# In-place normalization and ELU, fewer joint key-value rows in the second group, and a place per tile in a planned two-layer graph-attention kernel

## The chip, the cores and the metric

The kernel runs on one core of one Trainium2 chip, and the time is the device time of that core in microseconds (us). The engines are TensorE (PE in the profile, with its weight loads as PEld), VectorE (DVE), ScalarE (ACT), GpSimd (POOL) and SyncE (SP). POOL issues the DMAs that take their addresses from an index (gathers and scatters), SP issues the plain ones. All engines run their own instruction streams in order and meet at semaphores. "L870" means line 870 of the kernel before.

## What is computed

The input is `x` (8 batches of 2048 nodes with 256 features) and one 0/1 adjacency matrix of 2048 x 2048, in which a node has some 5 to 24 neighbours. Two layers follow each other, each wrapped as `x = layernorm(x + layer(x))`:

```python
# layer 0, 4 heads of 64; softmax inside chunks of 256 nodes
q, k, v = x @ Wq.T + bq, x @ Wk.T + bk, x @ Wv.T + bv
scores = where(mask == 0, -10, clip(q . k / 8, -10, 10))
ctx = sum over chunks of softmax(scores in the chunk) @ v
out = layernorm(ctx @ Wo.T + bo + x) * gamma + beta
# layer 1, graph attention
Wh = h @ W;  e = leaky_relu(a_src . Wh_i + a_dst . Wh_j, 0.2)
h_out = elu(softmax(where(adj, e, -inf)) @ Wh)
```

## The kernel before, in words

**Sparse form.** The first stage (`edge_lists`) reads the adjacency matrix, makes a list of neighbours for each node, and sorts the nodes by degree into 16 tiles of 128 nodes. A tile t has `CAPS[t]` slots, 24 for the first tile and 14 down to 5 for the others. A neighbour that is not among the slots has the constant score, and its share is put in by a correction. The batches are handled in two groups of four; group 0 and group 1 are called p=0 and p=1.

**Layer 0 of a group** begins with its tables (`tables`, L736 to L749): keys and values of all 16 row tiles are computed on PE, the keys evicted by DVE (L741), the values by ACT (L746), and both written to `kv_d[p]` by SP. A key row and its value row lie next to each other, 4096 bytes each. Only when all rows are written can the gathers of that group start. Then for each tile: `fetch_x` (a gather on POOL), `query` (PE, ACT), the gather of key rows, `scores0` (a product on DVE, L947, then transposes L960, an ACT copy L963 and a product with `sel` on PE, L967), `softmax0`, the gather of value rows, `context0` (each gathered row is weighed in place by its attention and the rows are summed on PE by transposes, L879), and `finish0` (output projection, two normalizations, the rows for layer 1, a write of x1 and a scatter of Wh).

**Joint rows.** For a few slots of a tile, key row and value row are fetched by one DMA of 8192 bytes a partition (`gather_both`, L840) in place of two of 4096 (L827). How many: `min(S_ % 2 + 2 * COMBO[p], S_)` of the `S_` slots. A joint row fills one buffer of the ring by itself, while two single rows share one. From among the joint rows `apart0` takes up to `SHARE[S_]`, and those are weighed by ACT, in 16 instructions of 64 columns (L861); all others are weighed by DVE (L870), two rows in one instruction of 2048 columns where they share a buffer, and one row of 1024 columns otherwise.

**Layer 1** gathers Wh rows for a tile (`fetch1`), makes the softmax, weighs and sums (`context1`), and ends with `finish1`: transposes on PE (L1138), ELU with an exp on ACT (L1142) and two DVE instructions (L1143, L1145), a normalization, and four scatters to the output (L1149). Tiles 0 to 7 are done for each group by itself, tiles 8 to 15 for both groups together. The eight single tiles of group 0 run interleaved with layer 0 of group 1.

**The order** is not written out by hand. Every operation is entered into a plan with an engine, an estimated cost, what it reads and writes, the buffers that it takes from a named room, and a due time; `schedule` then walks through the plan once, when the kernel is built, and on each engine starts the operation with the earliest due time that is ready and finds its buffers free. The result is the fixed order of each engine's instructions. The due times come from constants: `FIRST` and `WHENT` for the tables, one integer place per tile plus `WHEN0` for layer 0, `ORDB`, `ORDC`, `ORDJ` plus `WHEN1` and `WHENJ` for layer 1. Rooms that matter here: "u" with 7, later 14, ring buffers for two gathered rows each; "b" with 10 buffers of one row of 1040 floats; "x" with 18 small ones; "gr", a count of two loads of x1 under way.

**Buffers of the results.** `finish0` takes a new "b" buffer for its result (`o = pl.new("b")`), while the context lies in another (`cT`). `finish1` takes two new ones, `xr` for the x1 row and `y` for the result, while its context lies in `hT`.

Of the kernel before, what the change touches and what calls it, by code (L numbers as in the profile page):

```python
# [17 lines left out]
P = 128  # L18
# [22 lines left out]
GH = G * H  # L41
WW = GF + GH
EMIN = 4.5399929762484854e-05
RING, BIG, MID, WIDE, SMALL, BANKS, HALVES = 10, 10, 6, 4, 18, {"m": 2, "acc": 2}, {"al": 2, "pr": 1, "sc": 1}
PAIRS = 4
GATES = {"ga": 3, "gx": 2, "gq": 3, "gr": 2}
WHENT = (-24.15, 4.05)
WHEN0 = ((-4.55, -2.2, -1.95, -1.15, -0.85, -0.15, 0.1, 0.45, 4.85, -0.05, 0.8, 1.9, 2.1, 1.25, 3.9), (-2.15, -0.4,
         -1.35, -0.6, 0.6, -0.4, 0.75, 0.65, 1.15, 0.9, 0.9, 1.15, 2.1, 1.8, 3.55))
WHEN1 = ((-0.6, -0.5, -0.1, -0.15, 0.25, 0.4, 0.8, 2.35), (-1.4, -1.15, -1.05, -2.65, -0.7, -0.4, 1.25, 1.55))  # L50
NB = 32
ROWS = (3, 6, 9, 12)
DOTS = ((1, 3), ())
COMBO = (1, 1)
SHARE = {5: 0, 6: 0, 7: 2, 8: 2, 9: 2, 10: 2, 11: 2, 12: 2, 13: 3, 14: 4, 24: 4}
SHARE1 = {5: (), 6: (), 7: (1,), 8: (1,), 9: (2,), 10: (2,), 11: (2,), 12: (2,), 13: (2, 5), 14: (2, 5), 24: (2, 5, 8)}
JOINT = (8, 9, 10, 11, 12, 13, 14, 15)
SHAREJ = {9: (2, 4, 6), 8: (2, 4, 6), 7: (2, 4), 6: (2, 4), 5: (1, 3)}
WHENJ = (-1.4, -0.8, -0.45, -2.2, -0.7, -0.2, 0.65, 1.5, 0.95, 1.75)
ORDB = (2.5, 4.5, 6.5, 8.5, 10.5, 12.55, 14.5, 16.65)  # L60
ORDC = (3.85, 4.0, 7.3, 7.0, 6.7, 9.1, 11.5, 13.0)
ORDJ = (3.1, 5.4, 6.2, 7.8, 9.2, 10.35, 12.2, 13.95)
LATE = 4
FIRST = (-39.0, 2.0, 1.0, 0.0, -40.0, -31.25, -31.15, -38.6, 1.05)
COPY = (6.0, 12.0)
TUNED = ("FIRST", "WHENJ", "ORDB", "ORDC", "ORDJ")

# [36 lines left out]
class Plan:  # L106
# [43 lines left out]
    def schedule(self):  # L150
        import collections
        import heapq
        engines = ("PE", "DVE", "ACT", "POOL", "SP")
        cand = {e: [] for e in engines}
        free = {e: 0.0 for e in engines}
        for o in self.ops:
# [316 lines left out]
def sparse_path(ctx: ExitStack, tc: tile.TileContext, keep, x, adj, Wq, bq, Wk, bk, Wv, bv, Wo, bo, gamma, beta, W, a,  # L473
# [55 lines left out]
    def kept(name, shape, dt=F32):  # L529
        return Buf(phys=const.tile(shape, dt, name=name))  # L530
# [11 lines left out]
    xs = [kept(f"xs{p}", [P, GK, NT]) for p in range(NP)]  # L542
    shift = [kept(f"shift{p}", [P, KC, G]) for p in range(NP)]
    lift = [kept(f"lift{p}", [P, KC, G]) for p in range(NP)]
    room = ctx.enter_context(tc.tile_pool(name="room", bufs=1))
    for tag, n, shape in (("u", RING - 3, [P, UNIT, WW]), ("b", BIG, [P, WW]), ("s", MID, [P, 384]), ("h", WIDE, [P, 256]), ("x", SMALL, [P, 128])):
        pl.rooms[tag] = Room([room.tile(shape, F32, name=f"{tag}{k}") for k in range(n)], tag == "u")
# [256 lines left out]
              w=[(mv, k, k + 1)])  # L804
        return mv

    def normalized(dst, src, srcs, n=G):
        mv, nm = moments(src, srcs, n), pl.new("x")
        rs = rsqrt(mv, n, "y")
        V(C_TINY, lambda: nc.vector.scalar_tensor_tensor(nm.t[:, 0:n], mv.t[:, 0:2 * n].rearrange("p (b k) -> p b k", k=2)[:, :, 0],  # L810
                                                        -1.0, rs.t[:, 0:n], op0=ALU.mult, op1=ALU.mult), r=[mv, rs], w=[nm])
        for k in range(n):
            S(c_act(F, 2), lambda k=k: nc.scalar.activation(batches(dst)[:, k, :], src(k), AF.Identity, scale=rs.t[:, k:k + 1],  # L813
                                                            bias=nm.t[:, k:k + 1]), r=[srcs(k), rs, nm], w=[(dst, k, k + 1)])

    def flat(u):
        return u.t.rearrange("p s w -> p (s w)")
# [120 lines left out]
    def scores0(p, t):  # L938
        S_ = CAPS[t]
        q = got["q", p, t][1]  # L940
        units = got["k", p, t] + got["both", p, t]
        scs = [pl.new("sc")] + [pl.new("al") for _ in range(S_ > 16)]
        scv = lambda sl: scs[sl // 16].t[:, sl % 16 * GH:(sl % 16 + 1) * GH]
        for k, (u, items) in enumerate(units):
            slots, offs = [s for s, _, _ in items], [o for _, _, o in items]
            for o in offs:
                V(c_tt(GF), lambda u=u, o=o: nc.vector.tensor_tensor(  # L947
                    by_feature(flat(u)[:, o:o + GF], "j b"), by_feature(flat(u)[:, o:o + GF], "j b"), by_feature(q.t, "b j"), op=ALU.mult),
                  r=[q], w=[(u, o, o + GF)])
            if k in DOTS[p]:  # L950
                for s, o in zip(slots, offs):
                    V(55 + 1.06 * GF, lambda u=u, s=s, o=o: nc.vector.tensor_reduce(
                        scv(s), flat(u)[:, o:o + GF].rearrange("p (j e d) -> p e j d", j=NJ, d=DP), axis=AX.XY, op=ALU.add),
                      r=[(u, o, o + GF)], w=[(scs[s // 16], s % 16, s % 16 + 1)])
                continue
            pr, prT, m = pl.new("pr"), pl.new("h"), len(slots)
            for k, o in enumerate(offs):
                def turn(u=u, o=o, k=k, pr=pr):
                    for j in range(NJ):
                        nc.tensor.matmul(pr.t[:, k * P:(k + 1) * P], flat(u)[:, o + j * P:o + (j + 1) * P], ident,  # L960
                                         is_transpose=True, start=(j == 0), stop=(j == NJ - 1), skip_group_check=True)
                T(c_tr(8), turn, r=[(u, o, o + GF)], w=[(pr, k, k + 1)])
            S(c_act(m * P), lambda pr=pr, prT=prT, m=m: nc.scalar.copy(prT.t[:, 0:m * P], pr.t[:, 0:m * P]), r=[pr], w=[prT])  # L963

            def sums(prT=prT, slots=slots):
                for k, s in enumerate(slots):
                    nc.tensor.matmul(scv(s), prT.t[:, k * P:(k + 1) * P], sel, start=True, stop=True, skip_group_check=True)  # L967
            T(c_mm(m, 16), sums, r=[prT], w=[(scs[s // 16], s % 16, s % 16 + 1) for s in slots])
        st["s", p, t] = scs
# [41 lines left out]
    def finish0(p, t):  # L1011
        cT = st.pop(("c", p, t))
        (xg, gate), xT = got.pop(("x", p, t)), got.pop(("q", p, t))[0]
        o = pl.new("b")
        pos = []
        for half in range(2):
            po = pl.new("m")
# [15 lines left out]
        for b in range(G):  # L1033
            V(c_tt(F), lambda b=b: nc.vector.scalar_tensor_tensor(batches(o)[:, b, :], first(b), mv.t[:, 2 * b:2 * b + 1], gamma_r,
                                                                  op0=ALU.subtract, op1=ALU.mult), r=[pos[b // 2], mv, ga_b],
              w=[(o, b, b + 1)])
        rs = rsqrt(mv, G, "y")
        for b in range(G):
            V(c_tt(F), lambda b=b: nc.vector.scalar_tensor_tensor(batches(o)[:, b, :], batches(o)[:, b, :], rs.t[:, b:b + 1],
                                                                  batches(xg)[:, b, :], op0=ALU.mult, op1=ALU.add),  # L1040
              r=[rs, xg, gate], w=[(o, b, b + 1)], two=True)
        normalized(o, lambda b: batches(o)[:, b, :], lambda b: (o, b, b + 1))
        Q(lambda: nc.sync.dma_start(x1_d[p][t * P:(t + 1) * P, :], rows(o)), ROW, r=[o], w=[(x1_b[p], t, t + 1)])

        xT1, wh = pl.new("b"), pl.new("b")
# [85 lines left out]

    def finish1(p, t):
        hT = st.pop(("h", p, t))
        xr, y, gate = pl.new("b"), pl.new("b"), pl.new("gr")
        Q(lambda: nc.sync.dma_start(rows(xr), x1_d[p][t * P:(t + 1) * P, :]), ROW, r=[(x1_b[p], t, t + 1)], w=[xr, gate])
        for half in range(2):
            ph = pl.new("m")
            T(c_tr(4), lambda half=half, ph=ph: [nc.tensor.transpose(ph.t[:, c * P:(c + 1) * P], cols(hT)[:, 4 * half + c, :], ident)  # L1138
                                                 for c in range(4)], r=[(hT, 4 * half, 4 * half + 4)], w=[ph])
            hv = lambda b, half=half: b.t[:, 512 * half:512 * half + 512]  # L1140
            yk, xk = (y, 2 * half, 2 * half + 2), (xr, 2 * half, 2 * half + 2)
            S(c_act(512), lambda hv=hv, ph=ph: nc.scalar.activation(hv(y), ph.t, AF.Exp), w=[ph, yk])  # L1142
            V(601, lambda hv=hv, ph=ph: nc.vector.scalar_tensor_tensor(hv(xr), ph.t, 0.0, hv(xr), op0=ALU.max, op1=ALU.add),  # L1143
              w=[ph, xk])
            V(601, lambda hv=hv: nc.vector.scalar_tensor_tensor(hv(y), hv(y), 1.0, hv(xr), op0=ALU.min, op1=ALU.add),  # L1145
              r=[xk, gate], w=[yk])
        normalized(y, lambda b: batches(y)[:, b, :], lambda b: (y, b, b + 1))
        for b in range(G):
            Pq(C_DGE, lambda b=b: nc.gpsimd.indirect_dma_start(  # L1149
                out=out_v[t * B + p * G + b],  # L1150
                out_offset=bass.IndirectOffsetOnAxis(ap=nodeb.t[:, t, p * G + b:p * G + b + 1], axis=0),
                in_=batches(y)[:, b, :], in_offset=None), r=[(y, b, b + 1), nodeb], size=P * F * 4)

    for p, v0, dv in ((0, *FIRST[:2]), (1, *WHENT)):
        for c2 in range(NCH):
# [37 lines left out]
            pl.stage(v + w[6 + 2 * k], v + w[7 + 2 * k])  # L1193

    for k in range(NT):
        layer0(k, 0, k)
    early = [t for t in range(NT) if t not in JOINT]
    for k in range(NT):
        layer0(NT + k, 1, k)
    pairs_of = wj_d.rearrange("(n k) w -> n k w", k=NP)  # L1200
    for c in range(NT):
        Q(lambda c=c: nc.sync.dma_start(pairs_of[c * P:(c + 1) * P, 0, :], wh_d[c * P:(c + 1) * P, :]), 2 * P * WW * 4, r=[wh_b[0]],
# [438 lines left out]
```

## Time and profile before

| | us |
|---|---|
| median of the three runs | 2289.88 (2281.02 to 2292.70) |
| the profiled execution's own time | 2311.25 |
| its span, first to last instruction | 2309.5 |
| first key gather of group 0 | 214.85 |
| last scatter of layer 0, group 1 (L1063) | 1817.6 |

| engine | busy us | instructions | mean ns of one |
|---|---|---|---|
| PE matmul | 1830.4 | 12215 | |
| DVE | 1756.1 | 3262 | |
| ACT | 1184.1 | 4401 | |
| POOL | 1213.3 | 1160 | |
| L861, ACT weighing (all buffers) | 501.9 | 2016 | 345, and 249 from one to the next |
| L840, joint gathers | 80.1 | 80 | 1000 |

The DMA engines were busy for about 77% of the span and moved 275 GB/s on average. Times in the trace count from the first instruction. A row of the timeline gives the start, the length, the instruction and, in brackets, the engine's idle time before it and what ended that time. A row of the waits gives the waiting engine and line, what released it, and the total, the number and the longest of these waits. "Issue" stands for idle time without a visible cause.

### The profile page before, as it was taken

The page shows a single profiled execution, that of the slowest core. Times are in us where ns is not written, and L with a number is a line of the kernel's source. Part 1 is how long each engine was busy: PE and PEld are TensorE (multiplying, and loading weights), DVE is VectorE, ACT ScalarE, POOL GpSimd, SP SyncE. Part 2 cuts the span into 40 slices and gives each one's busy share as a digit, 9 for nine tenths or more (in the row PEclk, how much of TensorE's full clock was granted, in tenths as well). Part 3 has the DMA queues.
Part 4 walks back from the last instruction along what each step waited for, and adds up shares of the span by engine and source line. Part 5 has one row for each costly group of instructions (what it writes and reads, how often), then busy time and mean ns, then how long its engine had stood idle before and what let it go on. Part 6 is the DMA issues. An engine that isn't in the chain of part 4 may idle for free. (4 is left out here: it accounts for less than half of the span.)

```text
span 2309.5 us, 36948 instructions
## 1 busy us (share of the span) xinstructions
PE 1830.4 (79%) x12215; PEld 1627.8 (70%) x12215; DVE 1756.1 (76%) x3262; ACT 1184.1 (51%) x4401; POOL 1213.3 (53%) x1160
## 2 busy tenths in 40 slices
PE   6788699788887888897778888888988766776644
PEld 4577588677777777786767777787877656665534
DVE  8923367787888788877668878888887588878965
ACT  6633445235443545523344644555563658655656
POOL 6674114735454453457446564565554555665644
PEclk9899799989998999999889999999999878887767
DMA  8858578778887786766888888888887689978662
GB/s 304 296 188 293 199 249 287 291 261 301 304 281 277 269 309 242 264 234 226 312 330 313 290 310 300 285 310 292 310 293 267 225 307 353 322 289 318 208 217 81
DMA packets 187066, 635.56 MB, mean 275 GB/s; under 512 B 35082, under 2 KB 53388, under 8 KB 171120
## 3 DMA queue, kind: packets, MB, share of 16 engines
q0 software_dynamic: 137552, 505.18, 61.5%
q1 hardware_dynamic: 46608, 126.24, 14.9%
q10 hardware_dynamic: 2708, 1.71, 0.3%
q8 instruction: 99, 1.62, 0.3%
q14 instruction: 99, 0.81, 0.1%
HBM read 596.19 MB, written 109.71 MB: 306 GB/s over the span
## 5 line engine op out<-in xcount | busy, mean ns | idle before, releaser
L879 PE MATMUL acc<-ident,u 128*128 128x128 f32 x2856 | 384.1, 286 | 44.1 <-DVE u L870 29.1
L879 PEld LDWEIGHTS acc<-ident,u 128*128 128x128 f32 x2856 | 345.2, 150 | 60.3 <-DVE u L870 34.5
L861 ACT ACTIVATE u<-u,s 128x64 f32<-128x64 f32 x1344 | 333.1, 345 | 29.6 <-DVE s L1001 21.3
L870 DVE TENSOR_TENSOR u<-u,h 128x2048 f32<-128x2048 f32 (+1 forms) x175 | 321.3, 1849 | 0.3
L947 DVE TENSOR_TENSOR u<-u,q 128x1024 f32<-128x1024 f32 x224 | 264.3, 1209 | 46.0 <-PE q L682 27.7
L827 POOL DMA_INDIRECT u<-kv_d,idv x170 | 179.5, 1056 | 173.5 <-PE h L960 65.2
L827 POOL DMA_INDIRECT u<-kv_d,idk x168 | 171.9, 1023 | 178.9 <-PE h L960 64.2
L960 PE MATMUL h<-ident,u 128*128 128x128 f32 x1456 | 199.5, 286 | 26.8 <-DVE u L947 16.5
L960 PEld LDWEIGHTS h<-ident,u 128*128 128x128 f32 x1456 | 175.4, 151 | 36.3 <-DVE u L947 19.8
L963 ACT COPY h<-h 128x256 f32<-128x256 f32 (+1 forms) x172 | 56.8, 330 | 271.4 <-PE h L960 170.2
L1149 POOL DMA_INDIRECT out_dram<-b,nodeb x128 | 135.2, 1056 | 87.8 <-ACT b L813 54.2
L879 PE MATMUL acc<-ident,at 128*128 128x128 f32 x1208 | 157.9, 282 | 23.8 <-DVE at L870 16.8
L813 ACT ACTIVATE b<-b,x,x 128x256 f32<-128x256 f32 x256 | 136.3, 597 | 68.8 <-DVE x L810 52.6
L1055 PE MATMUL m<-wa,b 128*128 128x264 f32 x512 | 147.0, 427 | 25.8 <-ACT b L1061 10.5
L879 PEld LDWEIGHTS acc<-ident,at 128*128 128x128 f32 x1208 | 141.5, 146 | 29.0 <-DVE at L870 19.9
L967 PEld LDWEIGHTS h<-sel,h 128*128 128x128 f32 x546 | 82.3, 203 | 99.3 <-ACT h L963 60.4
L967 PE MATMUL h<-sel,h 128*128 128x16 f32 x546 | 85.0, 260 | 76.8 <-ACT h L963 47.0
L870 DVE TENSOR_TENSOR at<-at,h 128x2048 f32<-128x2048 f32 (+1 forms) x74 | 141.1, 1913 | 0.1
L947 DVE TENSOR_TENSOR at<-at,q 128x1024 f32<-128x1024 f32 x104 | 123.8, 1209 | 17.6 <-PE acc L879 6.5
L1027 PE MATMUL m<-wo,b 128*128 128x256 f32 x512 | 135.0, 387 | 2.8 <-issue 2.7
L929 PE MATMUL q<-wq,pair 128*128 128x256 f32 x512 | 135.4, 388 | 1.4 <-ACT pair L921 0.5
L1055 PEld LDWEIGHTS m<-wa,b 128*128 128x128 f32 x512 | 98.7, 209 | 47.0 <-issue 12.4
(232 smaller groups left out, 4276.7 us busy)
## 6 DMA issues: line engine op xcount, KB each, us to landing
kv_d<-b SPq DMA_DIRECT2D x64, 512.0 KB
at<-in_adj_dram SPq DMA_DIRECT2D x16, 1024.0 KB
x_d<-b SPq DMA_DIRECT2D x32, 512.0 KB
b<-x_d SPq DMA_DIRECT2D x32, 512.0 KB
b<-in_x_dram SPq DMA_DIRECT2D x24, 512.0 KB
xd_d<-b SPq DMA_DIRECT2D x24, 512.0 KB
wj_d<-wh_d SPq DMA_DIRECT2D x16, 520.0 KB
at<-in_x_dram SPq DMA_DIRECT2D x8, 512.0 KB
```

Of the source, the lines that this page charges most:

```text
L813: S(c_act(F, 2), lambda k=k: nc.scalar.activation(batches(dst)[:, k, :], src(k), AF.Identity, scale=rs.t[:, k:k + 1], bias=nm.t[:, k:k + 1 ...
L827: Pq(C_DGE, lambda u=u, o=o, s=s: nc.gpsimd.indirect_dma_start(out=flat(u)[:, o:o + size], out_offset=None, in_=table, in_offset=bass.Indi ...
L861: S(4 * C_WEIGH, lambda u=u, s=s, o=o, c=c, e=e, at=at: [nc.scalar.activation(flat(u)[:, o + h * D:o + (h + 1) * D], flat(u)[:, o + h * D: ...
L870: eng.tensor_tensor(pv, pv, av, op=ALU.mult)
L879: nc.tensor.matmul(quarters(accs[p][c // 4])[:, c % 4, :], flat(u)[:, o + c * P:o + (c + 1) * P], ident, is_transpose=True, start=not done ...
L929: nc.tensor.matmul(qb, cols(xT)[:, (2 * half + b) * KC + kc, :], wq[:, kc, :], start=(b == 0 and kc == 0), stop=False, skip_group_check=True)
L947: V(c_tt(GF), lambda u=u, o=o: nc.vector.tensor_tensor(by_feature(flat(u)[:, o:o + GF], "j b"), by_feature(flat(u)[:, o:o + GF], "j b"), b ...
L960: nc.tensor.matmul(pr.t[:, k * P:(k + 1) * P], flat(u)[:, o + j * P:o + (j + 1) * P], ident, is_transpose=True, start=(j == 0), stop=(j == ...
L967: nc.tensor.matmul(scv(s), prT.t[:, k * P:(k + 1) * P], sel, start=True, stop=True, skip_group_check=True)
L1027: nc.tensor.matmul(ob, cols(cT)[:, b * KC + kc, :], wo[:, kc, :], start=False, stop=(k == 1 and kc == KC - 1), skip_group_check=True)
L1055: nc.tensor.matmul(pw.t[:, 0:F + 2 * H], cols(xT1)[:, b * KC + kc, :], wa[:, kc, :], start=(kc == 0), stop=(kc == KC - 1))
L1149: Pq(C_DGE, lambda b=b: nc.gpsimd.indirect_dma_start(out=out_v[t * B + p * G + b], out_offset=bass.IndirectOffsetOnAxis(ap=nodeb.t[:, t, p ...
```

## The change

Five things are done. (1) `normalized` may write over its input; `finish0` puts its result over the context `cT`, and `finish1` over `hT`, so that they take one "b" buffer fewer each. In `finish1` the PE transposes now also wait for the load of the x1 row (`gate`). (2) `COMBO[1]` goes from 1 to 0: a tile of group 1 has two joint rows fewer, and so none or one. (3) Layer 0 of each tile gets a place of its own (`ORD0`, `ORD1`) in place of its number. (4) The other due times are set anew: `WHENT` (the tables of group 1 start at -22.35 and take 5.05 a pair of tiles, before -24.15 and 4.05), `FIRST`, `WHEN0`, `WHEN1`, `WHENJ`, `ORDB`, `ORDC`, `ORDJ`. (5) The room "x" gets 20 buffers. A second form of the normalization (`centred`) and sums on the way (`SUMS`) are added as well, but all entries of `SUMS` are 0, so that no instruction of theirs is made; `DOTS` only changes its form.

```diff
-RING, BIG, MID, WIDE, SMALL, BANKS, HALVES = 10, 10, 6, 4, 18, ...
+RING, BIG, MID, WIDE, SMALL, BANKS, HALVES = 10, 10, 6, 4, 20, ...
-WHENT = (-24.15, 4.05)
-WHEN0 = ((-4.55, -2.2, -1.95, -1.15, -0.85, -0.15, 0.1, 0.45, 4.85, ...
+WHENT = (-22.35, 5.05)
+WHEN0 = ((-10.5, -2.7, -2.05, -1.35, -0.85, -0.15, 0.1, 0.05, 2.2, ...
-COMBO = (1, 1)
+COMBO = (1, 0)
+SUMS = (0, 0, 0, 0)
-FIRST = (-39.0, 2.0, 1.0, 0.0, -40.0, -31.25, -31.15, -38.6, 1.05)
+FIRST = (-38.1, 0.5, 2.25, -0.7, -40.65, -31.75, -38.15, -43.75, 4.9)
+ORD0 = (0.0, 1.0, 2.0, ... 11.0, 12.45, 13.6, 13.85, 14.85)
+ORD1 = (16.6, 17.0, 18.0, ... 28.85, 30.6, 31.0)
...
     def normalized(dst, src, srcs, n=G, total=None):
...
-    ... bias=nm.t[:, k:k + 1]), r=[srcs(k), rs, nm], w=[(dst, k, k + 1)])
+    ... bias=nm.t[:, k:k + 1]), r=[rs, nm], w=[srcs(k)])
...
     def finish0(p, t):
-        o = pl.new("b")
+        o = cT
...
     def finish1(p, t):
-        xr, y, gate = pl.new("b"), pl.new("b"), pl.new("gr")
+        xr, y, gate = pl.new("b"), hT, pl.new("gr")
...
-            T(c_tr(4), ..., r=[(hT, 4 * half, 4 * half + 4)], w=[ph])
+            T(c_tr(4), ..., r=[(hT, 4 * half, 4 * half + 4), gate], w=[ph])
...
     for k in range(NT):
-        layer0(k, 0, k)
+        layer0(ORD0[k], 0, k)
     for k in range(NT):
-        layer0(NT + k, 1, k)
+        layer0(ORD1[k], 1, k)
```

## The prediction

> **What bounds the kernel now.** I read the page first: how busy each engine is over the span.
>
> ```profile
> span 2309.5 us, 36948 instructions
> ...
> PE 1830.4 (79%) x12215; PEld 1627.8 (70%) x12215; DVE 1756.1 (76%) x3262; ACT 1184.1 (51%) x4401; POOL 1213.3 (53%) x1160
> ```
>
> No engine is full: PE and DVE are close to each other and both stand idle for about a fifth of the span, 479 and 553 us. So I split the span at the points where the work changes (first key gather, first score, end of group 0's layer 0, end of group 1's) and took the table of busy times by stretch; behind the stretch and its length stand busy us (and instructions) of PE, PEld, DVE, ACT and POOL, then the granted clock, the DMA share and GB/s.
>
> ```profile
> 225.00:275.00 50.00, 30.32 (x136) 24.42 (x135) 7.39 (x10) 16.85 (x78) 11.89 (x12) 0.76 0.62 238
> 275.00:425.00 150.00, 142.31 (x923) 127.57 (x921) 110.53 (x111) 79.40 (x342) 57.23 (x44) 0.99 0.70 241
> 425.00:1000.00 575.00, 487.82 (x3233) 429.04 (x3232) 488.93 (x822) 255.91 (x975) 275.24 (x274) 0.93 0.79 282
> 1000.00:1200.00 200.00, 155.49 (x1143) 142.77 (x1142) 136.50 (x203) 76.58 (x286) 106.16 (x98) 0.90 0.78 283
> 1200.00:1817.00 617.00, 531.58 (x3791) 478.57 (x3789) 494.43 (x958) 327.76 (x1210) 338.37 (x336) 0.95 0.81 288
> 1817.00:2309.00 492.00, 307.93 (x2176) 281.82 (x2176) 385.02 (x831) 312.53 (x1069) 283.00 (x265) 0.77 0.73 267
> ```
>
> Each stage has another limit. From 225 to 275 DVE does 7 us of work. From 275 to 425 PE is full (95%) and DVE is not (74%): group 1's tables run there. From 425 to 1000 and from 1200 to 1817 both stand at 80 to 86%, so an engine there waits about a sixth of the time for the other. The changeover from group 0 to group 1 (1000 to 1200) is thin on both. At the end DVE leads with 78%.
>
> Then the timeline of PE in the first hole:
>
> ```profile
> 241.93 1.11 PE L676 MATMUL m<-ident,b 128*128 128x128 f32 x4 [9.85 <-issue]
> ...
> 246.97 2.15 PE L676 MATMUL m<-ident,pair 128*128 128x128 f32 x8 [0.20 <-ACT b L699]
> 253.97 3.74 PE L736 MATMUL m<-wkv,b 128*128 128x256 f32 x8 [4.84 <-ACT pair L921]
> ...
> 267.90 1.89 PE L736 MATMUL m<-wkv,pair 128*128 128x256 f32 x8
> 269.63 1.03 PE L929 MATMUL q<-wq,pair 128*128 128x256 f32 x4
> ```
>
> The keys of tile 0 are being gathered from 214.85 on and the ring is full by 240; the query transposes stand at 246.97; but eight groups of table matmuls of group 1 (L736) are ahead of the query product (L929). DVE's first score product starts at 275.04, and POOL waits 37.1 us, the longest of its waits for a buffer, until PE has read the first scored rows.
>
> **The change part by part.** The changed kernel's instruction order is fixed when it is built, so I counted in both orders.
>
> *The tables of group 1, later.* A group of table matmuls takes 1.73 us from start to start (266.18 to 267.90), a set of four transposes 0.44. Before the first score product PE had 16 groups and 12 sets of group 1's tables: 33 us; now 8 and 8: 17 us. Before the first score of tile 1 it is 95 against 73 us, of tile 5 118 against 100, of tile 9 125 against 120; from tile 11 on there is no difference. So the first score comes earlier by the eight groups, 13.8 us, and by the sixteen ACT activations ahead of the query's (4.8 us, 248.89 to 253.56 on ACT): about 18.6 us. The 9.85 us wait for the load of an x row stays, since one such transpose still stands ahead of the query. The same PE work comes back between tiles 1 and 11. Where PE is full it is given back wholly; from 425 on PE has 87 us of idle time and DVE 86, so some of it fills holes. Bounds: nothing, or all of the 50 us hole less the 13.8 us of work done in it, so 36. I take 15, near the 18.6 that the count gives. All other table operations move with these on DVE, ACT and SP; group 1's last table write is still ahead of the tenth of sixteen tiles' end on SP, far from its first gather, so it starts no new wait.
>
> *The changeover.* In the new order the last Wh scatter of group 0 is POOL's 484th operation, before the 511th, and on PE group 0 ends 35 operations earlier (815 of 1756, before 850 of 1772), because group 1's gathers and scores are not put ahead of it. Both engines have some 45 to 63 us idle in these 200. I take 5 us, between a loss of 10 and a gain of 20.
>
> *Fewer joint rows.* Two in each of 16 tiles, 32 rows. That adds 32 POOL gathers; the bytes stay. Of the rows that ACT weighed in group 1, 29, only 7 are left: 22 rows of 16 activations go, 352 instructions, at 249 ns from one to the next 87 us of ACT. DVE takes these 22 rows, and more of its rows sit in pairs: 16 instructions of 2048 columns more, 10 of 1024 fewer. Rows by form:
>
> ```profile
> L870 DVE TENSOR_TENSOR u<-u,h 128x2048 f32<-128x2048 f32 x105 | 238.4, 2275 | 0.1
> ...
> L870 DVE TENSOR_TENSOR u<-u,h 128x1024 f32<-128x1024 f32 x70 | 83.3, 1209 | 0.2
> ```
>
> From start to start these take 2.17 and 1.12 us in the chain, so DVE gains 34.7 - 11.2 = 23.5 us of work. It falls between 1120 and 1817, where DVE is idle for 123 us of the last 617. Its cover is the time in which DVE waits for PE; if that cover is gone, it costs 23.5. Against it: ACT answers sooner. PE waits 15 us there for ACT's score copies (L967 behind L963), and ACT itself stands still 21 times for more than 3 us (152 us over the span) without a cause among the other engines, about once in 210 of its 4401 instructions; 352 fewer make one or two of these stops of 7 us fewer. And a joint row no longer holds a ring buffer from its key's gather to the end of its context; POOL waited 48 and 35 us in 1117 to 1817 for PE to free buffers. I take a gain of 5, from +24 to -25.
>
> A rule speaks against splitting the rows. In the trace a gather takes 0.99 us of POOL and follows the next after 1.30; while 20 of 512 KB were issued back to back (214.85 to 239.57), the DMA engines moved 343 GB/s in the stretch from 225 to 250. The Trainium skill, "DMA: Bandwidth & Descriptors", section "Measured (HBM→SBUF, 128 partitions, SWDGE, issued from GpSimd)", says: batch DMAs to 1 MiB or more for at least 75% of peak, with 341 GB/s at 1 MB; its anatomy of one DMA gives a fixed 2.0 us for each. By the rule 32 halved transfers would cost 64 us one after the other; by the row they cost 32 x 1.30 = 42 us of POOL, which is idle for 45% of that stage, and no bandwidth, since the queue is deep. I take the row: nothing on the path.
>
> *Results in place.* No instruction goes or comes. A "b" buffer less is taken in each of 64 finishes, so x1 rows can be loaded earlier: in the SP queue's own waits three loads (L1135) wait 85 us for the DVE statistics that free one. The new wait sits on PE: the transposes of `finish1` wait for the x1 row, and behind them on PE are the next tile's sums (L879). Before, DVE took that wait (L1143), and its long waits, 47 us in all and 15.5 at most, name ACT's exp and not the load. So the row is there in time; if not, it costs PE up to such a wait at a few of 32 tiles. I take a gain of 5 at the end (from +10 to -15), by the order of the last stage together with these buffers: the same work stands behind the last scatter of layer 0 as before, 837 operations on DVE and 297 on PE. Two "x" buffers more: nothing.
>
> *Sum:* 15 + 5 + 5 + 5 = 30 us. The profiled execution's own time is 2311.25 (span 2309.5), 21 above the median of 2289.88; I read the gain off both: 2281 for a profile, 2260 for the median.
>
> **The rivals.** *The tables only change places (no change).* If PE bounds group 0 throughout, the 18.6 us at the start come back by tile 11, and new stops elsewhere take the rest: about 2290. For it: 95% PE from 275 to 425, 85% later, and that the summed work of PE is the same. Against it: 87 us of idle PE that is not needed as long as tables are at hand.
>
> *DVE becomes the bound of group 1 (slower).* The place is 1200 to 1817: DVE goes from 494 to 518 us of 617, 84%. If DVE can't get above about 80% because its inputs come late, each us more is a us of time: 2290 + 23.5 = 2313. It decides from the point where ACT's and the ring's relief stays under those 23.5 us and the start gains nothing. For it: DVE reached 88 to 90% in only a few hundred us in all. Against it: it did reach these, and PE is the fuller engine there.
>
> *The holes close (much faster).* With the full 36 us at the start, 20 in the changeover and 10 later: about 2225. For it: both holes are waits, not work. Against: other waits follow.
>
> **How the numbers follow.** The forecast has 0.57 and its own range is 2240 to 2278; no change 0.20, slower 0.16, much faster 0.07. About 0.5% is what a measurement of this kernel can tell from no change, here 2278 to 2301. The range for 8 in 10 reaches into both outer cases: 2225 to 2308. Faster 0.64, same 0.20, slower 0.16.
>
> **What would show it.** In the new profile: DVE's first score product some 17 us after the key ring fills and not 35; DVE busier than 74% in the 150 us after it; L861 with 1664 instructions; DVE some 23 us busier; POOL's longest ring wait under 25 us; PE waits at the transposes of `finish1` no longer than before. It is wrong if the end of group 0 comes no earlier, or if the stretch from there to the last Wh scatter of group 1 is longer than before.

## The result, and the profile after

The changed kernel takes 2257.07 us in the median of four runs (2247.56 to 2260.38); on the same chip the kernel before takes 2287.31 (2281.02 to 2292.70). The ratio is 0.986, with a 95% interval from 0.983 to 0.990: 30 us less. The prediction said 2260 and 30 us less.

The two profiled executions lie further apart than the medians: 2311.25 before, 2247.56 after, 64 us. The first is 24 us above its median, the second 10 below. So I split the 64 us with care, and use a second profile of the kernel before (2305.21) from another chip beside it. The page after begins so:

```profile
span 2245.8 us, 36611 instructions
...
PE 1807.6 (80%) x12215; PEld 1608.0 (72%) x12215; DVE 1766.8 (79%) x3262; ACT 1097.4 (49%) x4033; POOL 1242.8 (55%) x1192
```

DVE is 10.7 us busier and ACT 86.7 less busy than before; no engine is full, as before. Now the busy times of the kernel after in the first three of the stretches that the prediction showed (columns as there: PE, PEld, DVE, ACT, POOL, granted clock, DMA share, GB/s):

```profile
225.00:275.00 50.00, 40.75 (x214) 34.28 (x214) 33.40 (x34) 21.05 (x100) 10.00 (x10) 0.90 0.54 192
275.00:425.00 150.00, 133.04 (x881) 118.58 (x880) 99.98 (x106) 63.53 (x266) 71.06 (x58) 0.99 0.76 271
425.00:1000.00 575.00, 494.97 (x3303) 435.43 (x3302) 486.68 (x840) 274.82 (x1047) 264.06 (x264) 0.95 0.79 282
```

The hole is filled: DVE does 33 us of work from 225 to 275 where it did 7, and PE 41 where it did 30. The hole is also shorter, as PE's timeline after shows:

```profile
228.70 3.00 PE L742 MATMUL m<-wkv,pair 128*128 128x256 f32 x8 [3.56 <-issue]
231.66 2.62 PE L742 MATMUL m<-wkv,b 128*128 128x256 f32 x8
234.11 1.89 PE L742 MATMUL m<-wkv,pair 128*128 128x256 f32 x8
235.84 0.60 PE L682 MATMUL m<-ident,b 128*128 128x128 f32 x4
236.28 1.03 PE L953 MATMUL q<-wq,pair 128*128 128x256 f32 x4
```

The query product (L953, before L929) starts at 236.28 instead of 269.63, with few table groups (L742, before L736) ahead of it. POOL's waits for the ring follow at once. Behind PE's score transposes (L960 before, L985 after) they fall from 135.9 us in all and 37.1 at most to 77.7 and 7.0 (columns: us in all, times, longest; first before, then two rows of after):

```profile
POOL u L827 <- PE h L960: 135.9, 37, 37.1
```

```profile
POOL u L851 <- PE acc L903: 102.7, 57, 9.4
POOL u L851 <- PE h L985: 77.7, 35, 7.0
```

Then the span by stages. The cuts are the first key gather, the first score product, the last Wh scatter of group 0's layer 0 and that of group 1's. First the kernel before from its first score on, then after from its first gather on:

```profile
275.00:1117.60 842.60, 723.82 (x4876) 644.02 (x4874) 683.04 (x1057) 374.06 (x1453) 403.57 (x378) 0.94 0.76 268
1117.60:1817.60 700.00, 593.39 (x4209) 533.93 (x4207) 547.91 (x1036) 365.87 (x1363) 373.48 (x372) 0.94 0.83 295
1817.60:2309.50 491.90, 307.93 (x2176) 281.82 (x2176) 384.46 (x830) 312.25 (x1066) 282.97 (x265) 0.77 0.73 267
```

```profile
202.50:241.70 39.20, 28.36 (x120) 22.43 (x121) 5.96 (x11) 14.99 (x72) 19.92 (x20) 0.79 0.85 315
241.70:1041.70 800.00, 694.36 (x4623) 612.33 (x4622) 641.37 (x1008) 368.38 (x1439) 366.43 (x352) 0.96 0.77 274
1041.70:1790.40 748.70, 633.78 (x4537) 571.19 (x4537) 608.99 (x1093) 298.39 (x1052) 440.34 (x431) 0.94 0.83 291
1790.40:2245.80 455.40, 293.71 (x2176) 272.46 (x2176) 382.19 (x829) 309.31 (x1066) 284.64 (x265) 0.81 0.79 287
```

The first score comes 33 us earlier. Group 0's stage is 43 us shorter and group 1's 49 us longer, but the instruction counts say that this is mostly work moved across the cut: PE has 253 recorded instructions fewer in the first and 328 more in the second. PE's idle time (length less busy) falls by 13 us in the first and rises by 8 in the second. The last stage is 36 us shorter here with the same work, but in the second profile of before it takes 475.2 and not 491.9, so 17 of these 36 lie between two executions of one and the same kernel. What remains firm is the 33 us at the start; the other stages together give about nothing once the profiles are brought to their medians (33 against a difference of medians of 30).

### The profile page after: what moved, and what is told of

Same layout as the page of the kernel before. It is cut to its first block, busy times and chain, and to the rows that moved or that the text cites. A ratio compares the mean times of both kernels' runs of the same rounds, so it can differ in the third digit from the quotient of the medians.

```text
span 2245.8 us, 36611 instructions
## 1 busy us (share of the span) xinstructions
PE 1807.6 (80%) x12215; PEld 1608.0 (72%) x12215; DVE 1766.8 (79%) x3262; ACT 1097.4 (49%) x4033; POOL 1242.8 (55%) x1192
## 5 line engine op out<-in xcount | busy, mean ns | idle before, releaser
L903 PE MATMUL acc<-ident,u 128*128 128x128 f32 x2640 | 349.4, 283 | 67.9 <-DVE u L894 43.0
L903 PEld LDWEIGHTS acc<-ident,u 128*128 128x128 f32 x2640 | 311.4, 147 | 84.6 <-DVE u L894 50.6
L894 DVE TENSOR_TENSOR u<-u,h 128x2048 f32<-128x2048 f32 (+1 forms) x176 | 332.3, 1901 | 0.3
L972 DVE TENSOR_TENSOR u<-u,q 128x1024 f32<-128x1024 f32 x241 | 286.6, 1209 | 36.6 <-PE q L688 18.3
L851 POOL DMA_INDIRECT u<-kv_d,idv x194 | 207.5, 1070 | 190.4 <-PE acc L903 58.2
L851 POOL DMA_INDIRECT u<-kv_d,idk x206 | 206.8, 1004 | 180.0 <-issue 42.2
L885 ACT ACTIVATE u<-u,s 128x64 f32<-128x64 f32 x1056 | 259.3, 345 | 11.0 <-DVE s L1149 4.1
L985 PE MATMUL h<-ident,u 128*128 128x128 f32 x1568 | 202.8, 278 | 12.4 <-issue 4.8
L985 PEld LDWEIGHTS h<-ident,u 128*128 128x128 f32 x1568 | 181.3, 145 | 24.9 <-DVE u L972 8.9
L1082 PE MATMUL m<-wa,b 128*128 128x264 f32 x512 | 150.5, 430 | 27.2 <-issue 20.9
L894 DVE TENSOR_TENSOR at<-at,h 128x2048 f32<-128x2048 f32 (+1 forms) x82 | 154.1, 1886 | 0.1
L953 PE MATMUL q<-wq,pair 128*128 128x256 f32 x512 | 137.1, 391 | 7.8 <-issue 5.1
L972 DVE TENSOR_TENSOR at<-at,q 128x1024 f32<-128x1024 f32 x87 | 103.6, 1210 | 27.4 <-PE q L688 17.2
```

The lines of the kernel that those rows point to most:

```text
L851: Pq(C_DGE, lambda u=u, o=o, s=s: nc.gpsimd.indirect_dma_start(out=flat(u)[:, o:o + size], out_offset=None, in_=table, in_offset=bass.Indi ...
L885: S(4 * C_WEIGH, lambda u=u, s=s, o=o, c=c, e=e, at=at: [nc.scalar.activation(flat(u)[:, o + h * D:o + (h + 1) * D], flat(u)[:, o + h * D: ...
L894: eng.tensor_tensor(pv, pv, av, op=ALU.mult)
L903: nc.tensor.matmul(quarters(accs[p][c // 4])[:, c % 4, :], flat(u)[:, o + c * P:o + (c + 1) * P], ident, is_transpose=True, start=not done ...
L953: nc.tensor.matmul(qb, cols(xT)[:, (2 * half + b) * KC + kc, :], wq[:, kc, :], start=(b == 0 and kc == 0), stop=False, skip_group_check=True)
L972: V(c_tt(GF), lambda u=u, o=o: nc.vector.tensor_tensor(by_feature(flat(u)[:, o:o + GF], "j b"), by_feature(flat(u)[:, o:o + GF], "j b"), b ...
```

## The experiments

Times are compared as ratios to the kernel before on the same chip, because its median is 2287, 2323, 2295 and 2323 us on the chips used: the first beside the changed kernel, the second for t1 to t4, the third for t8 and t11 to t13, the last for t7, t10, t14 and t15. A comparison between these sets supposes that a ratio holds from chip to chip. The changed kernel itself was timed in one of them only, in four runs. "Seam wait" is PE's one wait just after the last Wh scatter of group 1; it is explained below.

| kernel | ratio (95%) | first score | end of group 0 | end of group 1 | span | seam wait |
|---|---|---|---|---|---|---|
| before | | 275.0 | 1117.6 | 1817.6 | 2309.5 | 13.1 |
| before, second profile (t13_before_again) | | 274.6 | 1131.7 | 1828.3 | 2303.5 | 12.4 |
| after | 0.986 (0.983 to 0.990) | 241.7 | 1041.7 | 1790.4 | 2245.8 | 13.6 |
| t1_times_only | 0.986 (0.984 to 0.989) | 241.4 | 1050.4 | 1824.3 | 2289.6 | 14.9 |
| t2_joint_only | 1.014 (1.010 to 1.018) | 273.7 | 1138.1 | 1884.8 | 2360.5 | 13.7 |
| t3_inplace_only | 1.006 (1.003 to 1.010) | 272.3 | 1125.3 | 1855.5 | 2328.6 | 35.8 |
| t4_joint_back | 0.989 (0.986 to 0.992) | 242.8 | 1048.6 | 1833.0 | 2303.4 | 12.0 |
| t8_start_times | 1.014 (1.010 to 1.018) | 245.9 | 1119.1 | 1850.8 | 2326.9 | 13.2 |
| t11_old_start | 1.028 (1.024 to 1.033) | 274.4 | 1111.5 | 1875.9 | 2351.6 | 14.9 |
| t12_dve_rows | 1.023 (1.018 to 1.027) | 274.4 | 1132.7 | 1878.1 | 2353.9 | 36.6 |
| t10_jitter | 1.008 (1.005 to 1.011) | 243.9 | 1050.0 | 1865.4 | 2334.0 | 35.5 |
| t14_before_jitter | 1.005 (1.003 to 1.007) | 274.3 | 1150.8 | 1862.9 | 2343.1 | 11.9 |
| t7_joint_dve | 0.996 (0.993 to 0.999) | 245.9 | 1051.7 | 1837.0 | 2310.9 | 14.5 |
| t15_integer_places | 1.004 (1.001 to 1.007) | 240.7 | 1123.8 | 1868.0 | 2331.0 | 35.2 |

The changed kernel also touches the planner, which its list of changes leaves out: it rounds each due time to six decimal places (`o.v = round(o.v, 6)`), so that due times that differ only in their last bits become equal, and then the operation that was entered first goes first. Put into the kernel before, this line alone moves 346 of the 1772 operations of PE to another place in the plan. All kernels that were made from the changed one have it: t1, t3, t4, t7, t10, t11 and t15.

My theory was that the due times carry the gain, by letting the first query pass the tables. The rivals were that the buffers freed by the results in place carry it, or that the joint rows do.

**The new times alone** (joint rows and buffers as before):

```diff
 # the kernel before, with all due times and places of the changed one
-WHENT = (-24.15, 4.05)
+WHENT = (-22.35, 5.05)
...
 COMBO = (1, 1)
```

> The kernel before with the new due times and places per tile alone: joint rows (1, 1), own result buffers, 18 small buffers. Theory (the order carries the gain: tables of group 1 later, changeover tighter): 2260 to 2270 us, and the first DVE score product at 240 to 258 us of the trace. Rival 1 (the freed b buffers make the order possible): 2280 to 2295. Rival 2 (fewer joint rows carry it): 2280 to 2295, with the first score as early as in the theory.

Measured 0.986, the same as the full change. The times, together with the rounding that this kernel keeps from the changed one, carry all of it: the gain needs neither the joint rows nor the results in place.

**The joint rows alone, with the old times:**

```diff
-COMBO = (1, 1)
+COMBO = (1, 0)
```

> The kernel before with two joint rows fewer in each tile of group 1, and nothing else. Theory: DVE gets 23.5 us more, ACT 87 less, POOL 42 more, together within 10 us of before, 2280 to 2298. Rival 2: 2260 to 2272. The slower rival of the prediction (DVE bounds group 1): 2305 to 2315.

Measured 1.014, 33 us slower. Its stage of group 1 takes 747 us, and not the 700 and 697 of the two profiles of before:

```profile
1138.10:1884.80 746.70, 613.44 (x4184) 553.03 (x4184) 559.90 (x1045) 295.41 (x1040) 402.02 (x401) 0.91 0.79 277
```

Against the row of before (1117.60:1817.60) PE idles 27 us more, and it is busy 20 us more with 25 instructions fewer, at a granted clock of 0.91 and not 0.94. Whether the clock is lower because PE waits more, or is a cost of its own, no run here separates.

**The results in place alone, with the old times:**

```diff
-        o = pl.new("b")
+        o = cT
...
-        xr, y, gate = pl.new("b"), pl.new("b"), pl.new("gr")
+        xr, y, gate = pl.new("b"), hT, pl.new("gr")
```

> The kernel before with the results written over their inputs, the wait for the x1 row on PE and 20 small buffers alone; old due times, old joint rows. Theory: a gain of about 5, 2277 to 2290. Rival 1: as the freed buffers need the new due times to be of use, no gain either, but the new due times without them (the other run) gain nothing. If the wait on PE is dear: 2295 to 2310.

Measured 1.006. Its seam wait is 35.8 us, 23 more than before, which is more than the whole loss of 14 us (0.6% of 2323). But the results in place do not stand alone here: the rounding is in this kernel too. With nothing but the rounding, the plan of the kernel before has the long wait at the seam already. The plan of t3 has the same order on PE up to the 1574th of 1772 operations, which lies behind the seam. So no gain is seen, and the 0.6% can't be put down to the results in place.

**The change with its joint rows put back:**

```diff
 # the changed kernel
-COMBO = (1, 0)
+COMBO = (1, 1)
```

> The changed kernel with the joint rows of before, (1, 1). Theory: within 10 us of the changed kernel, 2250 to 2267. Rival 2: 2275 to 2290. The slower rival's mechanism: faster than the changed kernel by up to 23 us, 2234 to 2250, as DVE has 23.5 us less to do in group 1.

Measured 0.989, against 0.986 with the cut. The intervals overlap, and the two come from different sets of runs: in the new order the cut of the joint rows is worth 0.2%, give or take 0.5, and so is not told from nothing.

**The start alone, and all but the start.** The theory needed these two.

```diff
 # t8: the kernel before;  t11: the changed kernel with the same lines put back
-WHENT = (-24.15, 4.05)
-WHEN0 = ((-4.55, -2.2, -1.95, -1.15, ...
-FIRST = (-39.0, 2.0, 1.0, 0.0, -40.0, -31.25, -31.15, -38.6, 1.05)
+WHENT = (-22.35, 5.05)
+WHEN0 = ((-10.5, -2.7, -2.05, -1.35, ...
+FIRST = (-38.1, 0.5, 2.25, -0.7, -40.65, -31.75, -38.15, -43.75, 4.9)
```

> The kernel before, with only the times of the start set anew: WHENT, FIRST and the first four times of a tile of group 0. Theory (the start carries the gain): the first score comes some 33 us earlier, as in the changed kernel, and the time is 0.986 to 0.990 of before. Rival (the start only changes places, the later times carry the gain): the first score comes as early, but group 0 ends no earlier, and the time is 0.996 to 1.004. Rival (any set of times that was not made for this order loses): 1.004 or more.

> The changed kernel, with the times of the start put back to those before: WHENT, FIRST and the first four times of a tile of group 0. Theory (the start carries the gain): the first score comes at about 275 us again, and the time is 0.996 to 1.004 of before. Rival (the later times carry it): 0.986 to 0.990. If both parts carry some: 0.990 to 0.996.

Measured 1.014 and 1.028. Both miss every simple theory: the start alone makes the kernel slower, and so does everything but the start (with the rounding, which t8 does not have). The start does what the count says (first score at 245.9, the gather at 204.2 and not 215.1), but then the rest is planned anew around it. Busy times of the two stages after it in t8_start_times:

```profile
245.90:1119.10 873.20, 740.75 (x4969) 662.20 (x4968) 690.25 (x1070) 385.55 (x1498) 410.27 (x379) 0.94 0.75 265
1119.10:1850.80 731.70, 601.10 (x4191) 539.32 (x4189) 546.01 (x1031) 365.52 (x1361) 372.96 (x372) 0.93 0.79 281
```

From its first score to the end of group 1 it takes 1605 us, against 1554 in t13_before_again (1828.3 less 274.6) on the same chip. Of these 51 us more, the first stage has 5 in PE's work (94 instructions that stood ahead of the first score before) and 11 in PE's idle time; the second has 9 in work, for about the same instructions, and 26 in idle time. The 29 us won are lost here and 22 more with them.

**DVE weighs the joint rows of group 1, nothing else changed:**

```diff
-        n = min(SHARE[CAPS[t]], len(got["both", p, t]))
+        n = min(SHARE[CAPS[t]], len(got["both", p, t]) if not p else CAPS[t] % 2)
```

> The kernel before, with its joint rows kept, but in group 1 the two that the cut would remove are weighed by DVE and no longer by ACT; POOL's gathers stay as they are. So the DVE part of the cut stands alone. DVE has at most 22 x 1.12 = 24.6 us more, ACT 352 instructions less. If DVE's load is what made the cut alone slower by 1.4%: 1.010 to 1.014 of before. If the 32 further gathers, or the order that follows from them, made it slower: 0.998 to 1.004. The forecast, that a relief of ACT covers it, would say 0.997 to 1.000.

Measured 1.023, more than any theory said; DVE is 22.4 us busier over the span (1777.5 against 1755.1), so DVE's time alone can't be the 50 us by which the spans differ. The seam wait is 24 us longer. The remainder of 26 is near DVE's 22, but nothing here shows that it is that.

**The kernel before once more, for its stages on this chip:**

> The kernel before, unchanged, for a profile of its stages on the same chip as the experiments: by all theories the first score near 275 us, the end of group 0 near 1118 to 1130 and the end of group 1 near 1818 to 1850, at a time within 1% of its median on this chip.

It answers in all points, with a shorter last stage (475.2).

By now five partial versions had lost time, most of them more than their own parts explain. A rival to all theories was left: each edit makes the planner write a new order, and the order itself has a price. So the next two kernels change nothing but the order:

```diff
 # t10: the changed kernel;  t14: the kernel before
-        layer0(NT + k, 1, k)
+        layer0(NT + k + 0.05 * (-1) ** k, 1, k)
```

(and the same in group 0; in the changed kernel the shift is added to `ORD0` and `ORD1`).

> The changed kernel, with each tile's place in layer 0 moved by 0.05 of a tile, up and down in turn. No work, no buffer and no stage changes, only who goes first where two operations are due at nearly the same time. If the gain lies in the stages (tables later, group 0 sooner out), it stays: 0.983 to 0.991 of before. If one exact order carries it (my reading of the partial edits, all slower by 0.6 to 2.8%): 0.995 to 1.015.

> The kernel before, with the same small shift of each tile's place. If a fresh order costs by itself what the partial edits cost: 1.008 to 1.020 of before. If those edits cost by what they do, and not by the new order: 0.996 to 1.004.

Measured 1.008 and 1.005. A shift of a twentieth of a tile takes away the whole gain of the changed kernel (1.008 against 0.986: 2.2%, 50 us, between two sets of runs), although its first score still comes at 243.9 and group 0 still ends at 1050. The kernel before loses 0.5%.

Where t10 loses is visible in one place. PE's timeline at the seam, first after, then t10_jitter:

```profile
1815.00 1.04 PE L903 MATMUL q<-ident,pair 128*128 128x128 f32 x8
1816.71 1.14 PE L1166 MATMUL m<-ident,b 128*128 128x128 f32 x8 [0.68 <-ACT b L911]
1831.41 1.97 PE L903 MATMUL acc<-ident,u 128*128 128x128 f32 x8 [13.55 <-DVE u L894]
```

```profile
1865.78 1.04 PE L903 MATMUL q<-ident,u 128*128 128x128 f32 x8
1867.49 1.14 PE L1166 MATMUL m<-ident,b 128*128 128x128 f32 x8 [0.68 <-ACT b L911]
1904.12 1.97 PE L903 MATMUL acc<-ident,at 128*128 128x128 f32 x8 [35.48 <-DVE at L894]
```

The last stage, layer 1 of both groups, can gather its rows only when the last Wh row of group 1 is scattered. From that scatter to the first weighed row pass some 40 us (1790.4 to 1831.4, and 1865.4 to 1904.1). After still has the sums of one single tile of layer 1 to do in that time: its PE lines up to 1815 belong to it. In t10_jitter that tile's sums are done by 1866, with the scatter, and nothing is left to cover the gathers: 2.6 us of PE work in 38.7, where after has 23.6 in 41.0 (first after, then t10_jitter).

```profile
1790.40:1831.41 41.01, 23.64 (x200) 23.06 (x201) 31.92 (x50) 27.24 (x108) 28.56 (x20) 0.82 0.96 371
```

```profile
1865.40:1904.12 38.72, 2.56 (x22) 2.02 (x20) 12.54 (x40) 6.27 (x16) 21.90 (x22) 0.58 0.90 352
```

The same is seen wherever it happens: four kernels (t3, t10, t12, t15) have some 2000 PE instructions after the last scatter, and a seam wait of 35 to 37 us; in the other ten profiles it is 2176 and 12 to 15 us. So the seam is a matter of 22 us of PE's waiting, and the order of one tile's sums decides it. It can stand for 22 of t10's 50 us, but no run changes the seam alone; and it is not the whole of any loss, since t2, t8 and t11 lose 1.4 to 2.8% with a short seam wait. For the other 28 us no single place was found: in group 1's stage PE idles 148 us in t10_jitter and 115 in after.

The plan itself shows much of this before any run. `schedule` ends with its own estimate of the time, made from its estimated costs:

| planned end, us | kernel and its measured ratio |
|---|---|
| 1973 | after 0.986 |
| 2006 to 2010 | t7 0.996, t1 0.986, t4 0.989 |
| 2015, 2020 | t15 1.004, t10 1.008 |
| 2029 | before |
| 2034 to 2036 | t11 1.028, t2 1.014, t8 1.014 |
| 2060 to 2081 | t14 1.005, t3 1.006, t12 1.023 |

All six kernels that were planned longer than the one before were slower, and four of the six that were planned shorter were faster. The sizes do not fit: from t4 to after the plan gains 36 us and the measurement 0.2%. The long wait at the seam is planned as well: in t3, t10, t12 and t15 the longest time there between the starts of two PE operations is 35 to 36 us in the plan, in all others 10 to 12. With the rounding alone the kernel before is planned at 2063 us, with 35 at the seam.

**DVE weighs the joint rows, in the new order:**

```diff
 # the changed kernel, COMBO = (1, 1), and
-        n = min(SHARE[CAPS[t]], len(got["both", p, t]))
+        n = min(SHARE[CAPS[t]], len(got["both", p, t]) if not p else CAPS[t] % 2)
```

> The changed kernel with its joint rows put back, but the two of each tile of group 1 weighed by DVE: the load of DVE rises as in the cut of joint rows, POOL's 32 further gathers go. If the DVE rows cost their 24 us in any order: 0.996 to 1.003 of before. If the new order covers them: 0.985 to 0.991. If every fresh order loses about 1%: 0.996 to 1.010, which would not be told from the first.

Measured 0.996. Between t4_joint_back (0.989) and this lies the move of the rows from ACT to DVE, and between this and after (0.986) lie the 32 further gathers. Read plainly, the DVE rows cost 0.8% and the gathers give 1.0% back. Both are below what a fresh order alone does in t10, so neither is shown. A cost of the further gathers is not seen.

**The places of the tiles put back:**

```diff
-ORD0 = (0.0, 1.0, 2.0, ... 11.0, 12.45, 13.6, 13.85, 14.85)
-ORD1 = (16.6, 17.0, 18.0, ... 28.85, 30.6, 31.0)
+ORD0 = (0.0, 1.0, 2.0, ... 12.0, 13.0, 14.0, 15.0)
+ORD1 = (16.0, 17.0, 18.0, ... 29.0, 30.0, 31.0)
```

> The changed kernel with the places of the tiles put back to 0, 1, 2 and so on; the start times, the joint rows and the results in place stay. 14 of the 32 places move, by 0.85 of a tile at most. If the start and the later times carry the gain: 0.984 to 0.991 of before. If the own place of each tile is a part of it: 0.992 to 1.000. If one exact order carries all: 0.995 to 1.015.

Measured 1.004. Group 0 ends 74 us later than in t10_jitter, and the stage holds the work of group 1 that the own places had put behind it:

```profile
240.70:1123.80 883.10, 745.20 (x4915) 660.74 (x4914) 685.54 (x1054) 371.31 (x1447) 412.81 (x382) 0.94 0.74 261
```

So it is the places in `ORD0` and `ORD1` that hold group 1's work back (PE has 4547 to 4623 instructions in this stage in all kernels with them, 4864 to 4969 in all others) and bring group 0's end forward. With the old start (t11) it ends at 1111.5, 20 us before t13_before_again. Of the 70 us by which that is later than in after, 33 are the start; in the stage PE then idles 26 us more and is busy 11 more, at a granted clock of 0.91 and not 0.96. Group 1's stage is then 71 us shorter than in t10 (744 against 815), and the totals are within 0.4%: an early end of group 0 is not by itself a gain.

## Why the prediction was right, and where not

The total and the sign are right: 30 us forecast, 30 measured. The sum is right only in part by its own steps, and that its total fits is luck: one term was half of what it measured, and the others were not found.

*The tables later (15; the count gave 18.6).* The mechanism is right, the size too small. From the first gather to the first score pass 39.2 us instead of 60.1: 20.9, near the count. The step left out that the new `FIRST` brings the first gather forward too, 214.9 to 202.5. That is 12 us more, seen in each kernel with the new start (201.7 to 206.7, with the old one 212.0 to 215.3). And the reading of the 9.85 us in the hole was wrong. I put it down to the load of an x row. On ACT's timeline of before the value copy for that bank runs late:

```profile
241.29 0.59 ACT L746 COPY b<-m 128x512 f32<-128x512 f32 x1 [14.31 <-remote]
```

It ends at 241.88 and the transposes start at 241.93; in the second profile the pair is 234.82 and 234.88. The transposes waited for the PSUM buffer that this copy frees. Why the copy was late stands in the last section.

That PE gives the start back where it is full did not happen in after and did in t8. The forecast saw the mechanism but had no means to tell which.

*The changeover (5, from -10 to +20).* A wait of 17 us of PE at 1100 is gone in all kernels with the new later times (none over 10 us in that stretch); its profile lines stand in the last section. It was PE's largest wait after the first score, in the changeover as the step had it. But it is gone in t2_joint_only too, which has the old times and is slower. So the new times are not shown to remove it, and in the stage times it does not stay visible as a gain.

*Fewer joint rows (5, from -25 to +24).* The counts are right: ACT's weighing has 1664 instructions (1056, 448 and 160 for the three kinds of buffers), and by its form

```profile
L894 DVE TENSOR_TENSOR u<-u,h 128x2048 f32<-128x2048 f32 x114 | 258.3, 2275 | 0.1
...
L894 DVE TENSOR_TENSOR u<-u,h 128x1024 f32<-128x1024 f32 x62 | 74.1, 1212 | 0.2
```

DVE's weighing (L870 and L894) over all its forms rises from 608.1 to 632.8 us, 24.7 for the 23.5 forecast; DVE as a whole is only 10.7 busier. The effect is not a gain of 5 but, in the new order, nothing that is measurable (t4), and a loss of 33 us in the old one (t2), which is outside the bounds given. The step that failed is the one about ACT's stops. ACT has 368 instructions less, yet it stands still for over 3 us without a named releaser 30 times (170 us) and not 21 (152 us). "One or two fewer" was drawn from a rate per instruction of ACT, and it took the stops for ACT's own. Most of them are waits for PE (16 of 21 before, 19 of 30 after; see the last section), which fewer instructions of ACT do not shorten.

*The rule on batching.* POOL is 29.5 us busier (42 were forecast with the pauses between gathers), the DMA engines moved 283 GB/s on average after 275, and the versions with joint rows in the new order, t4 and t7, are not faster than after. The prediction set against this the rule of the Trainium skill to batch DMAs to 1 MiB ("DMA: Bandwidth & Descriptors", "Measured (HBM→SBUF, 128 partitions, SWDGE, issued from GpSimd)"). Its 64 us were an estimate, 32 times the fixed 2.0 us that the same page gives under "Anatomy of one DMA — SWDGE (gpsimd) path". They would be 2.8% of the time, and no such cost is seen. A smaller one is not excluded, since the order alone moved the time by 2.2%.

*In place (5).* Not shown: nothing in the new order (t1 against t4), 0.6% slower with the old times, but there together with the rounding. The feared wait did not come. PE's waits at the transposes of `finish1` that name DVE are 17.5 us in 3 (before 37.0 in 15), those without a cause 24.5 (before 21.6).

*The checks.* The first score comes 13 us after the ring is full (229.0 to 241.7; 17 said). From 275 to 425 DVE is at 67% and not above 74%: what was to fill these 150 us was already done before 275. Its share from the first score on is what should have been named. POOL's longest wait for a buffer to gather into is 18.9 us (under 25 said). Group 0 ends 76 us earlier. But the stretch from there to the last Wh scatter of group 1 is longer, 749 against 700, and I had called the prediction wrong in that case. It was a bad test. It took the length of a stage between two events for the cost of its work, and 328 instructions of PE had changed sides.

*What the sum missed as a whole.* It added edits as if each kept its price. The three parts measure -1.4%, +1.4% and +0.6% (the first and the last with the rounding), which sum to +0.6%, and together they give -1.4%. Split the other way, the start alone gives +1.4% and all the rest +2.8%. With a planner each edit buys a new order, and the order's own price is up to 2% (t10). The rival that should have been there is this one: the same change in an order that does not fit it, at 1.5 to 3% slower. The total came out right because the count at the start was half of what it really gave, and the gains of 15 us in the other three steps were not found.

What stays open: which of the later times keeps the 33 us, where t10's 28 us beside the seam went, and what the rounding alone does to the measured time. It would take one order per constant, each with its own seam. No version was found that beats the changed kernel; t1_times_only is level with it.

## What to carry to other kernels

Where a planner or a scheduler orders the instructions, time a version with its priorities shifted by a hair as well; only what is larger than that scatter can be credited to an edit. Take care that a version with "one part alone" has nothing else in it that touches the order, be it a rounding, and read the planner's own estimate of the end beside the prediction. Look for the seams at which one stage's last write opens the next stage's first load, and see from the instruction counts on both sides whether something is left to cover it. And before a stage is called shorter, count its instructions: work may have moved over the line.

## What the runs showed of the hardware that was not expected

ACT's stops are for the most part waits for a late signal of PE. A stop here is idle time of over 3 us before which the profile names no instruction as the releaser: it writes "issue" or "remote". The kernel before has 21, and 16 of them carry "remote". By the trace's semaphore records each of these 16 ends 0.02 to 0.08 us after an update of one and the same semaphore, and only instructions of PE raise that one. The last of those had ended 1.6 to 16.6 us before the update, by the end that the profile models for it. In the second profile 19 of 23 stops end in this way, and in after 19 of 30. The profile names no releaser because the instruction and its signal lie so far apart.

The stops are also tied to places in the program. The two profiles of the kernel before are from different chips, and of the 21 stops in the first, 13 have a partner on the same line within 15 us in the second. The largest pair, with PE's last work ahead of it and PE's wait behind it, first of before and then of the second profile:

```profile
1081.36 1.94 PE L960 MATMUL h<-ident,u 128*128 128x128 f32 x16
...
1099.97 0.37 ACT L963 COPY h<-h 128x256 f32<-128x256 f32 x1 [12.80 <-remote]
...
1100.39 1.03 PE L967 MATMUL h<-sel,h 128*128 128x16 f32 x4 [17.08 <-ACT h L963]
```

```profile
1094.28 1.94 PE L960 MATMUL h<-ident,u 128*128 128x128 f32 x16
...
1114.03 0.37 ACT L963 COPY h<-h 128x256 f32<-128x256 f32 x1 [15.52 <-remote]
...
1114.46 1.03 PE L967 MATMUL h<-sel,h 128*128 128x16 f32 x4 [18.23 <-ACT h L963]
```

The profile says that PE waits here for ACT's copy. But the copy starts 0.02 to 0.03 us after PE's semaphore is raised, at 1099.94 and 1114.01, and PE's transposes end by their records at 1083.3 and 1096.2. So the time is lost between these records and the signal, and by the records both engines stand. The late value copy at 241.29 is of the same kind: the signal comes at 241.26, 9.2 us after the last end that is recorded for it. During the first stop the DMA engines are full:

```profile
1086.87:1099.97 13.10, 0.00 (x0) 0.00 (x0) 1.51 (x4) 0.30 (x2) 7.96 (x9) 0.50 1.00 387
```

Over all such stops the DMA share is 0.89 (before), 0.91 (second profile) and 0.92 (after), against about 0.77 over the span. I looked for instruction loading as the cause: packets of the instruction queues fall in 7 of the 21 stops of before, and in 6 to 16 of 21 stretches of the same length moved by 10 to 100 us. So that is not shown. What holds PE's signal back stays open: the transposes themselves can be late, since their ends are modelled, or the signal behind them. What is shown is that the stops go with late signals of PE, with busy DMA engines and with the place in the order, not with the number of ACT's instructions.
